# A deformable-convolution block: the sampling table stores a pixel and its step to the pixel below

## The chip, the cores and the metric

The kernel runs on one core of a Trainium2 chip. The metric is the device time of one execution in microseconds (us); lower is better. The median of nine executions of the kernel before is 8619.01 us, from 8593.27 to 8627.42 us. A profile is one further execution, taken by the hardware profiler. The names of the engines are those of the profile: PE is the matrix engine (PEld its weight loads), DVE the vector engine, ACT the scalar engine, POOL the engine that issues the indirect DMAs, SP the one that issues the plain DMAs.

## What is computed

The input is four images of 256 channels and 64 by 64 pixels in float32. The block first normalises over the channels and runs three modulated deformable 3x3 convolutions with a ReLU after each. The result is added to the input and goes through a mixture of eight experts, two per pixel. The change concerns the convolutions alone:

```python
om   = conv3x3(x, w_off) + b_off              # 27 numbers for each pixel
off  = om[:, :18].reshape(B, 9, 2, H, W); mask = sigmoid(om[:, 18:])
ys   = gy + base_y + off[:, :, 0];  xs = gx + base_x + off[:, :, 1]
y0, x0 = floor(ys), floor(xs);  wy, wx = ys - y0, xs - x0
# four gathered pixels, zero outside the image
v    = v00*(1-wy)*(1-wx) + v01*(1-wy)*wx + v10*wy*(1-wx) + v11*wy*wx
out  = relu(einsum('bikhw,oik->bohw', v * mask, w) + b)
```

For each of 9 taps and each pixel, 256 channels are read at a position between pixels, blended with bilinear weights and the mask, and multiplied by that tap's 256 by 256 weights.

## The kernel before

All data is float32. An image is worked in 8 blocks of 512 pixels (`BLK`), 8 image rows each; a block is 4 groups (`t`) of 128 pixels, one pixel per partition. The (layer, image) pairs are 12 stages: images 0 and 1 alternate through the three layers (stages 0 to 5), then images 2 and 3 (stages 6 to 11). So there are 96 blocks, 864 passes (block and tap `k`) and 3456 samples (block, tap and group).

**The table.** What is sampled lies in HBM as a table of (66 x 67) entries, one for each padded pixel. An entry has 512 numbers: the 256 channels of the pixel at (row, column) and, as its second half, those of the pixel one row below. Two entries that follow each other are therefore the four pixels of a bilinear sample. `store_table` (L160) writes a block with four DMAs from SP: for each half `d` of the rows, the pixels once as first halves and once, one row higher, as second halves. There are two tables per image parity, used by turns from layer to layer.

**Preparing.** `pre_block` (L170) loads 512 pixels of the input, transposes them (PE), normalises (DVE), stores the table, transposes back (PE) and copies into the padded image `xpad` (ACT). For images 0 and 1 this is the kernel's beginning; for images 2 and 3 its blocks are placed between the main blocks of stages 4 and 5. `off_block` (L197) runs the offset convolution from `xpad` on PE (L218), turns the result round (L231), and on DVE computes for 36 samples per pixel the table's index and four coefficients `cf` (L248 to L279). The off_block of a stage is placed between the main blocks of the stage ahead of it.

**The main block** (`main_block`, L281). For each tap and each group `t` (written a, b, c, d below), one indirect DMA from POOL (L296) brings two entries, 1024 numbers for each of 128 pixels, into one of 8 buffers `g`. ACT makes `s` by scaling the first 256 numbers (L303), one of 6 buffers. Three DVE multiply-adds of 256 numbers (`scalar_tensor_tensor`, L309) add the other three pixels. PE transposes `s` (L315) into a PSUM tile `tp`, of which there are 2. When the four groups of a tap are there, ACT copies them into `sT` in two instructions (L322), and PE multiplies with the tap's weights into the accumulator `acc` (L325). After nine taps ACT applies bias and ReLU (`r`, L335). In layers 0 and 1 DVE copies `r` into `xpad` (L338). PE transposes it back (`tpo`, L347, again a `tp` buffer), ACT copies that to `h` (L352, 2 buffers) and `store_table` writes the next layer's table. In layer 2 the input is added and `h` goes to HBM for the experts.

**The order.** Each engine works off its own list in order; the framework's scheduler makes the lists when the kernel is built, by priorities and its own estimates, so neighbouring taps overlap in it. In most passes of stages 0 to 3 and 6 to 11, DVE's list before has the three multiply-adds of a, then of b, c and d, and ACT's has the scaling of the next tap's a, then the two copies of L322, then the scalings of its b, c and d. In stages 4 and 5 the list of DVE mixes the samples for part of the taps (one multiply-add of a, one of b, and so on).

Of the kernel before, what the change touches and what calls it, by code (L numbers as in the profile page):

```python
# [14 lines left out]
P = 128  # L15
# [3 lines left out]
K = 9  # L19
# [71 lines left out]
def convolutions(ctx, tc, ins, x, B, dram, t_dram, ident, eps_c):  # L91
# [22 lines left out]
    for s in range(2):  # L114
        xp = cst.tile([P, CC, H + 2, W + 2], F32, name=f"xpad_{s}", tag=f"xpad_{s}")
        for c in range(CC):
            nc.vector.memset(xp[:, c, 0, :], 0.0)
            nc.vector.memset(xp[:, c, H + 1, :], 0.0)
            nc.vector.memset(xp[:, c, 1 : H + 1, 0:1], 0.0)
            nc.vector.memset(xp[:, c, 1 : H + 1, W + 1 : W + 2], 0.0)  # L120
        xpad.append(xp)
        for i in range(2):
            tb = dram.tile([TR * TC, 2 * C], F32, name=f"tab_{s}_{i}", tag=f"tab_{s}_{i}")
            v = tb.rearrange("(r c) (s f) -> r c s f", c=TC, s=2)
            nc.sync.dma_start(v[:, 0, :, :].rearrange("r s f -> r (s f)"), zero[:TR, : 2 * C])
# [43 lines left out]

    def pre_block(b, n):  # L170

        nm = f"pre_{b}_{n}"
        xc = work.tile([P, CC, BLK], F32, tag="xc", name=f"xc_{nm}")
        nc.sync.dma_start(xc, x[b, :, :, n * BLK : (n + 1) * BLK])
        tp = ps_t.tile([P, TPB, C], F32, tag="tp", name=f"tp_{nm}")
        for t in range(TPB):
            for c in range(CC):
                nc.tensor.transpose(
                    tp[:, t, c * P : (c + 1) * P], xc[:, c, t * P : (t + 1) * P], ident
                )  # L180
        h = work.tile([P, TPB, C], F32, tag="h", name=f"h_{nm}")
        normalise(nc, work, tp, h, eps_c, nm)
        store_table(table(0, b), h, n)
        tp2 = ps_t.tile([P, CC, BLK], F32, tag="tp", name=f"tp2_{nm}")
        for t in range(TPB):
            for c in range(CC):
                nc.tensor.transpose(
                    tp2[:, c, t * P : (t + 1) * P], h[:, t, c * P : (c + 1) * P], ident
                )
        for c in range(CC):  # L190
            nc.scalar.copy(
                rows(xpad[b % 2], c, n), tp2[:, c, :].rearrange("p (r w) -> p r w", w=W)
            )

    plans = {}

    def off_block(i, n):  # L197
# [6 lines left out]
        if n == 0:  # L204
            plans[i] = (
                work.tile([P, NB, J], I32, tag="idx", name=f"idx_{i}"),
                work.tile([P, NB, J, 4], F32, tag="cf", name=f"cf_{i}"),
            )
        idx, cf = plans[i]
        xp = xpad[b % 2]  # L210
# [64 lines left out]
        bm = small("bm", (P, J))  # L275
        nc.vector.tensor_tensor(bm, fr[:, 0, :], mk, ALU.mult)

        for q, (u, v) in enumerate(((am, om1), (bm, om1), (am, fr), (bm, fr))):
            nc.vector.tensor_tensor(cf[:, n, :, q], u, v[:, 1, :], ALU.mult)  # L279

    def main_block(i, n):  # L281
        l, b = stages[i]
# [5 lines left out]
        for k in range(K):  # L288
            tp = ps_t.tile([P, CC, BLK], F32, tag="tp", name=f"tp_{nm}_{k}")
            for t0 in range(0, TPB, 2):  # L290

                gs, ss = [], []
                for t in (t0, t0 + 1):
                    j = t * K + k
                    g = gat.tile([P, 4 * C], F32, tag="g", name=f"g_{nm}_{j}")
                    nc.gpsimd.indirect_dma_start(  # L296
                        out=g,
                        out_offset=None,
                        in_=tb,
                        in_offset=bass.IndirectOffsetOnAxis(ap=idx[:, n, j : j + 1], axis=0),  # L300
                    )
                    s = smp.tile([P, C], F32, tag="s", name=f"s_{nm}_{j}")
                    nc.scalar.activation(s, g[:, :C], AF.Copy, scale=cf[:, n, j, 0:1])  # L303
                    gs.append(g)
                    ss.append(s)
                for q in range(1, 4):
                    for u in range(2):
                        j = (t0 + u) * K + k
                        nc.vector.scalar_tensor_tensor(  # L309
                            ss[u], gs[u][:, q * C : (q + 1) * C], cf[:, n, j, q : q + 1], ss[u],  # L310
                            ALU.mult, ALU.add,
                        )
                for u in range(2):
                    for c in range(CC):
                        nc.tensor.transpose(  # L315
                            tp[:, c, (t0 + u) * P : (t0 + u + 1) * P],
                            ss[u][:, c * P : (c + 1) * P],
                            ident,
                        )
            sT = smT.tile([P, CC, BLK], F32, tag="sT", name=f"sT_{nm}_{k}")  # L320
            for c in range(CC):
                nc.scalar.copy(sT[:, c, :], tp[:, c, :])  # L322
            for c in range(CC):
                for o in range(CC):
                    nc.tensor.matmul(  # L325
                        acc[:, o, :],
                        lhsT=wk[:, k, c, o * P : (o + 1) * P],
                        rhs=sT[:, c, :],
                        start=(k == 0 and c == 0),
                        stop=(k == K - 1 and c == CC - 1),  # L330
                    )
# [19 lines left out]
        for t in range(0, TPB, 2):  # L351
            nc.scalar.copy(h[:, t : t + 2, :], tp[:, t : t + 2, :])  # L352
# [390 lines left out]
```

## Time and profile before

| | |
|---|---|
| time, median of 9 | 8619.01 us |
| time of the profiled execution | 8636.17 us |
| its span, first to last instruction | 8634.2 us |
| mean granted PE clock | 0.906 of full speed |
| beginning, to the first `sT` copy | 0 to 181 us |
| stages 0 to 11 | 181 to 6331 us |
| experts | from 6331 us |
| a stage of 72 passes, such as stage 1 (680 to 1176 us) | 496 us |
| stage 4 (2169 to 2756 us), stage 5 (2757 to 3331 us) | 587 us, 574 us |
| busy: PE, DVE, ACT, POOL | 6646.1, 5757.8, 3085.9, 4397.0 us |

The profile's page gives for each engine its busy time and how it is spread over 40 slices of the span, the granted PE clock and the DMA engines' load in the same slices, and the costliest groups of instructions. A group's row gives line, engine, operation, result and operands, shapes and count; then its total busy time and the mean duration of one in ns; then how long the engine stood idle just before such instructions and what ended that. The timeline lists instructions of a window: start, length, engine, line, and in brackets the idle time before and what ended it. Neighbours of one group are merged (xN). The waits are inferred from semaphores. Durations include the tail in which the result is written, so the next independent instruction can start before an instruction ends.

### The profile page before, as it was taken

What the parts mean: (1) busy time and instruction counts of PE and PEld (TensorE: products, weight loads), DVE (VectorE), ACT (ScalarE), POOL (GpSimd) and SP (SyncE); (2) the same over time, 40 slices, a digit from 0 to 9 for tenths busy, and PEclk for the clock granted to TensorE, in tenths of its full rate; (3) what the DMA queues carried; (4) which work ended last, traced back from release to release, by engine and by line L of the source; (5) the groups of instructions that cost most, each with busy time, mean ns of one, the idle gap of its engine ahead of it and who ended that gap; (6) DMA issues with size and microseconds to landing.
All of it is one profiled execution on the core that took longest, in us unless ns stands there. A gap on an engine that the chain in (4) does not pass through costs nothing.

```text
span 8634.2 us, 93574 instructions
## 1 busy us (share of the span) xinstructions
PE 6646.1 (77%) x25984; PEld 3678.5 (43%) x25984; DVE 5757.8 (67%) x14852; ACT 3085.9 (36%) x6658; POOL 4397.0 (51%) x4289
## 2 busy tenths in 40 slices
PE   7888888888877878888888888787753928658285
PEld 3434334433443433333343443343332827547274
DVE  5888888888777777888888887788862323323122
ACT  3444444444444444444444444444421212112011
POOL 1555565655555555555555555555523243433434
PEclk9999999999988889999999999889966969879697
DMA  7899999999888888999999999999932224333243
GB/s 234 315 326 318 325 334 322 323 319 326 309 294 295 302 295 319 325 323 327 318 335 324 319 322 336 347 327 326 321 140 80 92 93 129 113 100 121 82 128 122
DMA packets 791203, 2245.78 MB, mean 260 GB/s; under 512 B 131848, under 2 KB 244488, under 8 KB 789144
## 3 DMA queue, kind: packets, MB, share of 16 engines
q0 software_dynamic: 567168, 1917.26, 63.2%
q1 hardware_dynamic: 223512, 322.54, 11.1%
q8 instruction: 207, 3.39, 0.2%
q14 instruction: 316, 2.59, 0.1%
HBM read 2154.08 MB, written 231.78 MB: 276 GB/s over the span
## 4 chain that ended last, share of the span: by engine, by line
PE 38%; DVE 18%; issue 17%; DMA 15%; ACT 9%; POOL 2%; another core or an unknown queue 1%; ACTq 0%; SPq 0%; POOLq 0%; DVEq 0%
PE acc L325 15%; DVE s L309 15%; DMA g<-tab,idx 6%; PE tp L315 5%; DMA zs<-z,slots 5%; PE po L218 5%; PE ph L611 5%; PE py L626 4%; ACT sT L322 4%; ACT s L303 3%; DMA w<-in_W,wrow 3%; PE tpo L347 1%; POOL gy L650 1%; DMA gy<-ys,slots 1%
## 5 line engine op out<-in xcount | busy, mean ns | idle before, releaser
L309 DVE SCALAR_TENSOR_TENSOR s<-g,cf,s 128x256 f32<-128x256 f32 x10368 | 4711.6, 484 | 1049.2 <-ACT s L303 562.6
L296 POOL DMA_INDIRECT g<-tab,idx x3456 | 3586.1, 1038 | 2732.3 <-DVE s L309 1556.2
L325 PE MATMUL acc<-sT,wk 128*128 128x512 f32 x6912 | 3445.1, 645 | 405.4 <-ACT sT L322 317.1
L325 PEld LDWEIGHTS acc<-sT,wk 128*128 128x128 f32 x6912 | 1334.9, 203 | 2169.4 <-issue 1441.1
L322 ACT COPY sT<-tp 128x512 f32<-128x512 f32 x1728 | 927.7, 590 | 2516.8 <-PE tp L315 2195.3
L303 ACT ACTIVATE s<-g,cf 128x256 f32<-128x256 f32 x3456 | 1529.9, 510 | 394.7 <-DMA g<-tab,idx 241.9
L315 PE MATMUL tp<-ident,s 128*128 128x128 f32 x6912 | 1079.2, 284 | 434.2 <-DVE s L309 412.3
L315 PEld LDWEIGHTS tp<-ident,s 128*128 128x128 f32 x6912 | 819.2, 144 | 1159.8 <-DVE s L309 643.9
L585 POOL DMA_INDIRECT w<-in_W,wrow x312 | 312.2, 1001 | 858.4 <-ACT hT L620 341.7
L218 PE MATMUL po<-xpad,wo 128*32 128x512 f32 x3456 | 675.9, 610 | 1.9 <-DMA wo<-in_conv_w_off 1.0
L620 ACT ACTIVATE hT<-ph,w 128x256 f32<-128x256 f32 x624 | 258.7, 470 | 1164.2 <-PE ph L611 1080.5
L611 PE MATMUL ph<-fzT,w 128*128 128x256 f32 x2496 | 593.2, 393 | 65.2 <-DMA w<-in_W,wrow 64.7
L626 PE MATMUL py<-w,hT 128*128 128x256 f32 x2496 | 593.3, 393 | 57.4 <-DMA w<-in_W,wrow 45.1
L600 PE MATMUL ftp<-ident,zt 128*128 128x128 f32 x624 | 96.5, 284 | 619.6 <-DMA zt<-zs 610.1
L611 PEld LDWEIGHTS ph<-fzT,w 128*128 128x128 f32 x2496 | 483.9, 197 | 154.6 <-DMA w<-in_W,wrow 83.7
L626 PEld LDWEIGHTS py<-w,hT 128*128 128x128 f32 x2496 | 479.4, 197 | 134.7 <-issue 51.6
L572 POOL DMA_INDIRECT zs<-z,slots x256 | 251.6, 983 | 489.2 <-DMA zs<-z,slots 351.4
L634 DVE TENSOR_TENSOR y<-py,w 128x512 f32<-128x512 f32 x156 | 107.7, 691 | 490.2 <-PE py L626 448.5
L604 DVE COPY fzT<-ftp 128x512 f32<-128x512 f32 x156 | 107.5, 690 | 426.7 <-PE ph L611 272.5
L600 PEld LDWEIGHTS ftp<-ident,zt 128*128 128x128 f32 x624 | 76.9, 148 | 634.8 <-DMA zt<-zs 612.0
L650 POOL DMA_INDIRECT gy<-ys,slots x256 | 245.9, 960 | 148.4 <-issue 67.2
L658 DVE SCALAR_TENSOR_TENSOR facc<-gy,cw,facc 128x256 f32<-128x256 f32 x256 | 120.3, 483 | 222.1 <-DMA gy<-ys,slots 176.3
(122 smaller groups left out, 2567.0 us busy)
## 6 DMA issues: line engine op xcount, KB each, us to landing
tab<-h SPq DMA_DIRECT2D x256, 256.0 KB
g<-tab,idx POOLq DMA_INDIRECT x3456
zt<-zs SPq DMA_DIRECT2D x156, 256.0 KB
ys<-y SPq DMA_DIRECT2D x156, 256.0 KB
tab<-h_pre SPq DMA_DIRECT2D x128, 256.0 KB
zs<-nil SPq DMA_DIRECT2D x12, 1664.0 KB
xc_pre<-in_x SPq DMA_DIRECT2D x32, 512.0 KB
xr<-in_x SPq DMA_DIRECT2D x32, 512.0 KB
```

The source lines that it names most:

```text
L218: nc.tensor.matmul(po[g * Q : (g + 1) * Q, :], lhsT=wo[:, k, c, :], rhs=xp[:, c, RPB * n + ky : RPB * n + ky + RPB, kx : kx + W], start=(m ...
L296: nc.gpsimd.indirect_dma_start(out=g, out_offset=None, in_=tb, in_offset=bass.IndirectOffsetOnAxis(ap=idx[:, n, j : j + 1], axis=0),)
L303: nc.scalar.activation(s, g[:, :C], AF.Copy, scale=cf[:, n, j, 0:1])
L309: nc.vector.scalar_tensor_tensor(ss[u], gs[u][:, q * C : (q + 1) * C], cf[:, n, j, q : q + 1], ss[u], ALU.mult, ALU.add,)
L315: nc.tensor.transpose(tp[:, c, (t0 + u) * P : (t0 + u + 1) * P], ss[u][:, c * P : (c + 1) * P], ident,)
L322: nc.scalar.copy(sT[:, c, :], tp[:, c, :])
L325: nc.tensor.matmul(acc[:, o, :], lhsT=wk[:, k, c, o * P : (o + 1) * P], rhs=sT[:, c, :], start=(k == 0 and c == 0), stop=(k == K - 1 and c ...
L585: nc.gpsimd.indirect_dma_start(out=w, out_offset=None, in_=ins[src], in_offset=bass.IndirectOffsetOnAxis(ap=st["wrow"][:, f : f + 1], axis=0),
L611: nc.tensor.matmul(ph[:, h, :], lhsT=w1[:, o : o + P], rhs=zT[:, c, :], start=(c == 0), stop=(c == CC - 1),)
L620: nc.scalar.activation(hT[:, h0 + h, :], ph[:, h, :], AF.Gelu, bias=w1[:, k : k + 1])
L626: nc.tensor.matmul(py[:, u, :], lhsT=hT[:, h, u * P : (u + 1) * P], rhs=w2[:, h * C : (h + 1) * C], start=(h == 0), stop=(h == HC - 1),)
L650: nc.gpsimd.indirect_dma_start(out=g, out_offset=None, in_=ys[b % 2], in_offset=bass.IndirectOffsetOnAxis(ap=st["slots"][:, i, m : m + 1], ...
```

## The change

The second half of a table entry now holds the difference, pixel below minus pixel, in place of the pixel below. A sample then is: one multiply-add of 512 numbers that gives both columns' values at the fractional row (`v0 + wy * step`, written over `g`), one scaling of the left column on ACT by `(1-wx)*mask`, and one multiply-add of 256 numbers that adds the right column times `wx*mask`. There are three coefficients in place of four.

The differences are made by the new `store_steps`: a DVE subtraction over `xpad` (128 x 1024), eight transposes on PE into a `tp` buffer, two copies on ACT into a buffer of `h`'s pool, and the two DMAs that `store_table` no longer makes. It is called after `pre_block` has filled `xpad` and after the main blocks of layers 0 and 1, 32 + 64 = 96 times. In an image's last block it also makes the last row's step (minus the pixel), 12 times.

```diff
-            nc.sync.dma_start(v[H, 1 : W + 1, 1, :], zero[:W, :C])
...
-    def store_table(tb, h, n):
+    def store_table(tb, h, n, s):
         v = tb.rearrange("(r c) (s f) -> r c s f", c=TC, s=2)
         for d in range(2):
             src = h[d * W : (d + 1) * W, :, :]
-            for s in range(2):
-                r0 = RPB * n + d + 1 - s
-                dst = v[r0 : r0 + RPB - 1 : 2, 1 : W + 1, s, :]
-                nc.sync.dma_start(dst.rearrange("t x f -> x t f"), src)
+            r0 = RPB * n + d + 1 - s
+            dst = v[r0 : r0 + RPB - 1 : 2, 1 : W + 1, s, :]
+            nc.sync.dma_start(dst.rearrange("t x f -> x t f"), src)
+
+    def store_steps(tb, xp, n, nm):
+        dd = work.tile([P, CC, BLK], F32, tag="xc", name=f"dd_{nm}")
+        nc.vector.tensor_tensor(
+            dd.rearrange("p c (r w) -> p c r w", w=W),
+            xp[:, :, 1 + RPB * n : 1 + RPB * (n + 1), 1 : W + 1],
+            xp[:, :, RPB * n : RPB * (n + 1), 1 : W + 1],
+            ALU.subtract,
+        )
+        tp = ps_t.tile([P, TPB, C], F32, tag="tp", name=f"tpd_{nm}")
+        for t in range(TPB):
+            for c in range(CC):
+                nc.tensor.transpose(
+                    tp[:, t, c * P : (c + 1) * P], dd[:, c, t * P : (t + 1) * P], ident
+                )
+        hd = work.tile([P, TPB, C], F32, tag="h", name=f"hd_{nm}")
+        for t in range(0, TPB, 2):
+            nc.scalar.copy(hd[:, t : t + 2, :], tp[:, t : t + 2, :])
+        store_table(tb, hd, n, 1)
+        if n == NB - 1:
...
+            nc.sync.dma_start(v[H, 1 : W + 1, 1, :], hl[:W, 0, :])
...
-        store_table(table(0, b), h, n)
+        store_table(table(0, b), h, n, 0)
...
+        store_steps(table(0, b), xpad[b % 2], n, nm)
...
-        om1 = small("om1")
-        nc.vector.tensor_scalar(om1, fr, -1.0, 1.0, ALU.mult, ALU.add)
+        om1 = small("om1", (P, J))
+        nc.vector.tensor_scalar(om1, fr[:, 1, :], -1.0, 1.0, ALU.mult, ALU.add)
...
-        am = small("am", (P, J))
-        nc.vector.tensor_tensor(am, om1[:, 0, :], mk, ALU.mult)
-        bm = small("bm", (P, J))
-        nc.vector.tensor_tensor(bm, fr[:, 0, :], mk, ALU.mult)
-        for q, (u, v) in enumerate(((am, om1), (bm, om1), (am, fr), (bm, fr))):
-            nc.vector.tensor_tensor(cf[:, n, :, q], u, v[:, 1, :], ALU.mult)
+        nc.vector.tensor_copy(cf[:, n, :, 0], fr[:, 0, :])
+        nc.vector.tensor_tensor(cf[:, n, :, 1], om1, mk, ALU.mult)
+        nc.vector.tensor_tensor(cf[:, n, :, 2], fr[:, 1, :], mk, ALU.mult)
...
+                    v = g.rearrange("p (x s f) -> p x s f", x=2, s=2)
+                    nc.vector.scalar_tensor_tensor(
+                        v[:, :, 0, :], v[:, :, 1, :], cf[:, n, j, 0:1], v[:, :, 0, :],
+                        ALU.mult, ALU.add,
+                    )
                     s = smp.tile([P, C], F32, tag="s", name=f"s_{nm}_{j}")
-                    nc.scalar.activation(s, g[:, :C], AF.Copy, scale=cf[:, n, j, 0:1])
+                    nc.scalar.activation(s, v[:, 0, 0, :], AF.Copy, scale=cf[:, n, j, 1:2])
...
-                for q in range(1, 4):
-                    for u in range(2):
-                        j = (t0 + u) * K + k
-                        nc.vector.scalar_tensor_tensor(
-                            ss[u], gs[u][:, q * C : (q + 1) * C], cf[:, n, j, q : q + 1], ss[u],
-                            ALU.mult, ALU.add,
-                        )
+                for u in range(2):
+                    j = (t0 + u) * K + k
+                    nc.vector.scalar_tensor_tensor(
+                        ss[u], gs[u][:, 1, 0, :], cf[:, n, j, 2:3], ss[u], ALU.mult, ALU.add
+                    )
...
-            store_table(table(l + 1, b), h, n)
+            store_table(table(l + 1, b), h, n, 0)
+            store_steps(table(l + 1, b), xpad[b % 2], n, nm)
```

The lists that are built for the changed kernel, with A for the new 512-wide multiply-add, S for the scaling, B for the 256-wide multiply-add and T for the two copies of `sT`: in the later taps of most blocks DVE has A of a, A of b, B of a, B of b, A of c, B of c, A of d, B of d, and ACT has S of a, b, c, d and then T, so the next tap's S of a stands behind T. After a main block of layers 0 and 1 (that is, during tap 0 of the next block) ACT's list has the two copies of `h`, S of b of tap 1, the two copies of `hd`, then T of tap 0.

More of the change, by code (lines that the diff above doesn't have):

```diff
@@ L164, in store_table @@
             src = h[d * W : (d + 1) * W, :, :]
-            for s in range(2):
-                r0 = RPB * n + d + 1 - s
-                dst = v[r0 : r0 + RPB - 1 : 2, 1 : W + 1, s, :]
-                nc.sync.dma_start(dst.rearrange("t x f -> x t f"), src)
+            r0 = RPB * n + d + 1 - s
[20 more added lines that the diff above has]
+        if n == NB - 1:
+            dl = work.tile([P, CC, W], F32, tag="dl", name=f"dl_{nm}")
+            nc.vector.tensor_scalar(dl, xp[:, :, H, 1 : W + 1], -1.0, None, ALU.mult)
+            tp = ps_t.tile([P, TPB, C], F32, tag="tp", name=f"tpl_{nm}")
+            for c in range(CC):
+                nc.tensor.transpose(tp[:W, 0, c * P : (c + 1) * P], dl[:, c, :], ident)
+            hl = work.tile([P, TPB, C], F32, tag="h", name=f"hl_{nm}")
+            nc.scalar.copy(hl[:W, 0, :], tp[:W, 0, :])
+            v = tb.rearrange("(r c) (s f) -> r c s f", c=TC, s=2)
+            nc.sync.dma_start(v[H, 1 : W + 1, 1, :], hl[:W, 0, :])
     def pre_block(b, n):
@@ L206, in off_block @@
                 work.tile([P, NB, J], I32, tag="idx", name=f"idx_{i}"),
-                work.tile([P, NB, J, 4], F32, tag="cf", name=f"cf_{i}"),
+                work.tile([P, NB, J, 3], F32, tag="cf", name=f"cf_{i}"),
             )
@@ L301, in main_block @@
                     )
+                    v = g.rearrange("p (x s f) -> p x s f", x=2, s=2)
[3 more added lines that the diff above has]
+                    )
                     s = smp.tile([P, C], F32, tag="s", name=f"s_{nm}_{j}")
-                    nc.scalar.activation(s, g[:, :C], AF.Copy, scale=cf[:, n, j, 0:1])
-                    gs.append(g)
+                    nc.scalar.activation(s, v[:, 0, 0, :], AF.Copy, scale=cf[:, n, j, 1:2])
+                    gs.append(v)
                     ss.append(s)
-                for q in range(1, 4):
-                    for u in range(2):
-                        j = (t0 + u) * K + k
-                        nc.vector.scalar_tensor_tensor(
-                            ss[u], gs[u][:, q * C : (q + 1) * C], cf[:, n, j, q : q + 1], ss[u],
-                            ALU.mult, ALU.add,
-                        )
+                for u in range(2):
[3 more added lines that the diff above has]
+                    )
                 for u in range(2):
```

## Prediction

> **What bounds the kernel now.** I read the page first, for the shares and the groups, then the busy time by stage, then the timeline of an undisturbed pass and of the two kinds of block ends.
>
> ```profile
> DVE  5888888888777777888888887788862323323122
> ...
> PEclk9999999999988889999999999889966969879697
> DMA  7899999999888888999999999999932224333243
> ...
> L309 DVE SCALAR_TENSOR_TENSOR s<-g,cf,s 128x256 f32<-128x256 f32 x10368 | 4711.6, 484 | 1049.2 <-ACT s L303 562.6
> L296 POOL DMA_INDIRECT g<-tab,idx x3456 | 3586.1, 1038 | 2732.3 <-DVE s L309 1556.2
> ```
>
> Up to 6331 us DVE and the DMA engines are both near nine tenths. POOL waits for DVE (1556.2 us, for free `g` buffers), and L303's wait for gathers is only 241.9 us in all, so the DMA engines are full but gathers are seldom late. Where PEclk drops, PE's matmuls set the pass; the change does not touch those. Whether DVE's work bounds a pass is shown by the timeline (start, length, engine, line; count last).
>
> ```profile
> 3606.82 1.01 DVE L309 SCALAR_TENSOR_TENSOR s<-g,cf,s 128x256 f32<-128x256 f32 x2
> 3608.49 5.89 DVE L309 SCALAR_TENSOR_TENSOR s<-g,cf,s 128x256 f32<-128x256 f32 x12 [0.66 <-ACT sT L322]
> 3615.03 1.06 DVE L309 SCALAR_TENSOR_TENSOR s<-g,cf,s 128x256 f32<-128x256 f32 x2 [0.66 <-ACT sT L322]
> ```
>
> ```profile
> 3606.97 1.07 ACT L322 COPY sT<-tp 128x512 f32<-128x512 f32 x2 [3.88 <-PE tp L315]
> 3607.93 1.71 ACT L303 ACTIVATE s<-g,cf 128x256 f32<-128x256 f32 x4
> 3613.52 1.07 ACT L322 COPY sT<-tp 128x512 f32<-128x512 f32 x2 [3.88 <-PE tp L315]
> 3614.48 1.71 ACT L303 ACTIVATE s<-g,cf 128x256 f32<-128x256 f32 x4
> ```
>
> A pass is 6.55 us (3606.97 to 3613.52). It is a ring: T (the two copies), S (scalings), DVE's samples, transposes, T. DVE works 5.89 us of it and waits 0.66 us, each time for ACT. So DVE's work counts only as far as the ring shrinks.
>
> **Durations.** A 256-wide multiply-add lasts 484 ns; two on the same `s` start 0.52 us apart (1.01 us for two), two independent ones 0.40 (an independent pair takes 0.88 us at 1316.03). A sample of three is so 0.52 + 0.52 + 0.40 = 1.44 us. S lasts 0.51, the next starts 0.40 later. The trace has no 512-wide multiply-add out of SBUF. DVE's subtraction of 1024 numbers (L344) takes 1221 ns: (1221 - 484) / 768 = 0.96 ns a number, so A = 484 + 256 x 0.96 = 0.73 us. Ends: 0.69 (L634, 512-wide, 691 ns) and 0.97 (two of 484); I take 0.73, from the two rows of the same kind of operands.
>
> **The pass in the later taps (5 to 8), stages 0-3 and 6-11.** T at 0. Before, by those rows: S of b ends at 1.48, b's first multiply-add starts at 1.51, d's last ends at 5.92, and T comes 0.58 after that (3612.94 to 3613.52): 6.50, measured 6.55. After, S of a stands behind T and starts at 0.96 (A of a and b are done by then), ends 1.48; B of a 1.51, B of b 1.91, A of c 2.31 to 3.05, S of c to 3.59, B of c 3.62 to 4.11; A of d 4.02 to 4.76, S to 5.30, B 5.33 to 5.82; T at 6.40. The 0.39 us of DVE time saved per sample does not come out: samples c and d now hand over DVE to ACT to DVE, and nothing lies under that. 0.10 us x 4 passes x 80 blocks = **-32 us**. Ends: A at 0.97 makes two serial A's 0.24 longer each, +0.38 a pass; A at 0.69 makes it -0.18. The hand-over DVE to ACT I took as the 0.03 us of ACT to DVE (3615.00 to 3615.03); PE to ACT takes 0.09 (3613.43 to 3613.52), and with that the pass is 6.52.
>
> The Trainium skill (Perfetto Trace Analysis, Optimizing Scalar/DVE Operations) says larger operations pay if the engine is saturated, but that breaking instructions up may finish work sooner where the engine is not saturated and causes bubbles elsewhere. The second half speaks against this change in c and d: DVE idles while ACT scales, and by it A split in two would let S start about 0.25 us earlier twice, an estimate of 5.9 us a pass where the sum above has 6.40.
>
> **Ends of blocks in layers 0 and 1 (64).** Before:
>
> ```profile
> 3516.11 1.26 ACT L335 ACTIVATE r<-acc,bk 128x512 f32<-128x512 f32 x2 [2.11 <-PE acc L325]
> ...
> 3518.45 1.07 ACT L352 COPY h<-tpo 128x512 f32<-128x512 f32 x2 [0.67 <-PE tpo L347]
> 3519.41 1.09 ACT L322 COPY sT<-tp 128x512 f32<-128x512 f32 x2
> ```
>
> `r` ends at 3517.37; the two copies to `xpad` on DVE (429 ns) end about 3518.2. Added: subtraction 1.22 on DVE, eight transposes on PE (0.60 for four, so 1.04), copies of `hd` 1.07 on ACT. T of tap 0 stands behind `hd` and so comes near 3521.7, +2.2 us. Queued behind `hd` on ACT are T and the S's, and DVE's B's wait for those. Against it: the next passes (6.23, 7.4 and 6.65 us now) find A's done ahead, and DVE then needs only 4 x 1.05 = 4.2 us in them; PE needs 3.69 (eight L325) plus transposes and offset matmuls, about 5.3. They can win back 1 to 4 us. I take **0** per block, from -2 to +2.2: -128 to +141 us. It also takes a third `tp` tile per block end; that is in the +2.2.
>
> **Stages 4 and 5 (16 blocks).** These already last 587 and 574 us instead of 496, because a prepared block sits in each.
>
> ```profile
> 2458.84 0.30 ACT L82 ACTIVATE sd_pre<-mv_pre,eps_c 128x4 f32<-128x4 f32 x1 [1.54 <-DVE mv_pre L80]
> 2462.07 1.07 ACT L191 COPY xpad<-tp_pre 128x512 f32<-128x512 f32 x2 [2.93 <-PE tp_pre L187]
> 2463.03 0.92 ACT L303 ACTIVATE s<-g,cf 128x256 f32<-128x256 f32 x2
> 2463.84 1.07 ACT L322 COPY sT<-tp 128x512 f32<-128x512 f32 x2
> ```
>
> Subtraction, transposes and `hd` now come between the `xpad` copy and T of tap 0: 2463.14 + 1.22 + 1.04 + 1.07 + hand-overs = 2466.6 in place of 2463.84, +2.8 us. The later passes there take 5.5 us now,
>
> ```profile
> 2435.50 1.07 ACT L322 COPY sT<-tp 128x512 f32<-128x512 f32 x2 [3.23 <-PE tp L315]
> 2436.46 1.31 ACT L303 ACTIVATE s<-g,cf 128x256 f32<-128x256 f32 x3
> 2440.99 1.07 ACT L322 COPY sT<-tp 128x512 f32<-128x512 f32 x2 [3.23 <-PE tp L315]
> ```
>
> because the list mixes samples and the 0.40 us distance counts; the new list has the serial c and d of 6.40 us: +0.9 x 4. Together 6.4 x 16 = **+102 us**; ends 2.8 (gathers set those passes anyway) and 12 (`hd`, third tenant of two `h` buffers here, also waits for the store of the main block's `h`): +45 to +190.
>
> **The beginning (16 prepared blocks in 181 us).** The same chain, 3.3 us each, partly beside other blocks, with the `h` and `xc` buffers shared: 2.5 x 16 = **+40 us**, 0 to +56.
>
> **Small parts.** `hl`, 12 times, waits on ACT for the store of the same block's `h`: 1.5 us each, **+18**, 0 to +60. DVE's three fewer small operations per off_block (about 0.2 us, 96 times) lie in DVE's gaps: 0, down to -58. SP's DMAs keep number and bytes (half leave after `hd`, and the next stage but one reads them); one zero store per table goes. POOL's gathers keep number and bytes; a buffer comes free, as now, with its sample's last multiply-add.
>
> **Sum.** -32 + 0 + 102 + 40 + 18 = +128. Profiled execution: 8636.17 + 128 = 8764. It stood 17 above the median of the runs, so the predicted time is 8747 us.
>
> **Rivals.** *DVE's saving comes out (faster).* DVE's work falls by 10368 x 0.484 - 3456 x (0.73 + 0.484) = 822 us of durations, less 117 for 96 subtractions. For: DVE is 88% busy and POOL waits for it. Against: the list order above. It decides if taps 1 to 4 keep a run-ahead and take about 5.8 us: -0.8 x 4 x 80 = -256, so 8747 - 256 = about 8490.
> *The hand-overs or a tail cost more.* With 0.09 instead of 0.03 and one extra wait of that kind, +0.18 us in each of 864 passes: +155, about 8900.
> *The 512-wide one costs like two (0.97).* +0.48 a pass over my 6.40, on 864 passes: +415, about 9160.
> *Gathers set the time anyway.* Bytes are unchanged, and the DMA share in the stages is 0.92: within 0.2%, 8619. Against: L303's small wait for gathers.
>
> **How the numbers follow.** Chances: my sum 0.57, saving comes out 0.18, hand-overs 0.12, width 0.06, gathers 0.07. About 0.2% (17 us) is what a measurement tells from no change. Of the 0.57, 0.55 lies above that: slower 0.73, same 0.09, faster 0.18. The sum's own range from its ends is 8640 to 8900; with half of the faster case and the hand-overs the range is 8540 to 8940.
>
> **What would show it.** Right: A near 730 ns, DVE busy lower by some 600 us yet with more idle behind L335 (the new scaling); passes of 5 to 8 at 6.4 to 6.5 us; tap 0's T two us later; stages 4 and 5 longer by 50 us each. Wrong: passes at 5.8 or less in the later taps (hand-overs overlap after all), or A near 0.97.

## The result, and the profile after

The changed kernel takes 8684.92 us (median of 10 runs, 8660.53 to 8697.73); the kernel before took 8620.64 us beside it (8593.27 to 8641.05). The ratio is 1.0076, interval 1.0066 to 1.0086: slower by 64 us, where 128 were forecast. On a second chip (below) the ratio is 1.0098, interval 1.0081 to 1.0115. The profiled execution took 8707.08 us, span 8705.1, granted clock 0.905 as before.

From the page of the changed kernel: busy tenths of DVE and of the DMA engines, then groups (busy time, mean ns of one, idle time before them and what ended most of it).

```profile
DVE  4677767776666666777777777566661323323122
...
DMA  5899999999888888999999999999942224333243
...
L323 POOL DMA_INDIRECT g<-tab,idx x3456 | 3628.0, 1050 | 2761.7 <-DVE s L340 1818.7
...
L340 DVE SCALAR_TENSOR_TENSOR s<-g,cf,s 128x256 f32<-128x256 f32 x3456 | 1608.7, 483 | 1659.6 <-ACT s L335 1395.6
L330 DVE SCALAR_TENSOR_TENSOR g<-g,cf 128x512 f32<-128x512 f32 x3456 | 2519.8, 746 | 91.0 <-DMA g<-tab,idx 82.5
L335 ACT ACTIVATE s<-g,cf 128x256 f32<-128x256 f32 x3456 | 1679.9, 511 | 1930.8 <-DVE g L330 1423.7
```

The change did what its words say: A (L330, the 512-wide multiply-add) lasts 746 ns, B (L340) 483, and DVE is busy 5058.9 us in place of 5757.8. But 699 us less work bought nothing. DVE's idle time behind ACT's scaling (S) rose from 562.6 to 1395.6 us, and ACT's scalings now wait 1423.7 us for the multiply-add A, where the kernel before shows 55.5 us of waiting for DVE at its scalings. The timeline of a pass of the later taps (start, length, engine, line) shows the two waits facing each other, first DVE:

```profile
3652.89 0.88 DVE L340 SCALAR_TENSOR_TENSOR s<-g,cf,s 128x256 f32<-128x256 f32 x2 [0.77 <-ACT sT L352]
3653.69 0.75 DVE L330 SCALAR_TENSOR_TENSOR g<-g,cf 128x512 f32<-128x512 f32 x1
3655.01 0.48 DVE L340 SCALAR_TENSOR_TENSOR s<-g,cf,s 128x256 f32<-128x256 f32 x1 [0.57 <-ACT s L335]
3655.41 0.74 DVE L330 SCALAR_TENSOR_TENSOR g<-g,cf 128x512 f32<-128x512 f32 x1
3656.73 0.48 DVE L340 SCALAR_TENSOR_TENSOR s<-g,cf,s 128x256 f32<-128x256 f32 x1 [0.58 <-ACT s L335]
```

then ACT in the same pass:

```profile
3651.38 1.07 ACT L352 COPY sT<-tp 128x512 f32<-128x512 f32 x2 [1.10 <-issue]
3652.34 0.92 ACT L335 ACTIVATE s<-g,cf 128x256 f32<-128x256 f32 x2
3654.47 0.51 ACT L335 ACTIVATE s<-g,cf 128x256 f32<-128x256 f32 x1 [1.22 <-DVE g L330]
3656.19 0.51 ACT L335 ACTIVATE s<-g,cf 128x256 f32<-128x256 f32 x1 [1.21 <-DVE s L340]
3657.80 1.07 ACT L352 COPY sT<-tp 128x512 f32<-128x512 f32 x2 [1.11 <-issue]
```

The pass is 6.42 us (3651.38 to 3657.80) against 6.55 before. A of c ends at 3654.44, S of c runs from 3654.47 to 3654.98, B of c starts at 3655.01: 0.03 us each way, with nothing on DVE in between. DVE idles 0.77 + 0.57 + 0.58 us of the pass.

The end of a block, ACT's part of it:

```profile
3675.03 1.26 ACT L365 ACTIVATE r<-acc,bk 128x512 f32<-128x512 f32 x2 [0.78 <-PE acc L355]
...
3678.23 1.07 ACT L382 COPY h<-tpo 128x512 f32<-128x512 f32 x2 [0.27 <-PE tpo L377]
...
3680.25 1.07 ACT L185 COPY hd<-tpd 128x512 f32<-128x512 f32 x2
3681.38 1.07 ACT L352 COPY sT<-tp 128x512 f32<-128x512 f32 x2
```

From `r` to the copies of tap 0 (T) it was 3.30 us in the block end that the prediction shows, and is 6.35 in this one. Where the time of the two profiled executions lies, by the first `sT` copies of the stages:

| | before | after | difference |
|---|---|---|---|
| beginning, to the first T | 181.1 | 262.1 | +81.0 |
| stages 0 to 3 and 6 to 9 | 3970.7 | 3952.0 | -18.7 |
| stages 4 and 5 | 1162.9 | 1197.1 | +34.2 |
| stages 10 and 11 | 1017.5 | 993.0 | -24.5 |
| after the last T | 2302.0 | 2300.9 | -1.1 |

In layer 2 (stages 10 and 11), where no steps are made, the change gains; it loses where the steps of layer 0 are made, in the beginning and in stages 4 and 5.

### The profile page after: what moved, and what is told of

It is laid out like the page before. It is cut to its first block, busy times and chain, and to the rows that moved or that the text cites. A ratio compares the mean times of both kernels' runs of the same rounds, so it can differ in the third digit from the quotient of the medians.

```text
span 8705.1 us, 91686 instructions
## 1 busy us (share of the span) xinstructions
PE 6745.2 (77%) x26776; PEld 3762.3 (43%) x26776; DVE 5058.9 (58%) x11216; ACT 3349.3 (38%) x6860; POOL 4439.9 (51%) x4289
## 4 chain that ended last, share of the span: by engine, by line
PE 25%; issue 13%; DMA 10%; ACT 8%; DVE 7%; POOL 2%; another core or an unknown queue 0%; ACTq 0%; POOLq 0%; SPq 0%; DVEq 0%
PE acc L355 9%; ACT s L335 5%; DMA zs<-z,slots 5%; PE ph L642 4%; PE py L657 4%; DVE g L330 3%; DMA w<-in_W,wrow 3%; PE tp L345 2%; PE po L248 2%; ACT sT L352 2%; DVE s L340 1%; DMA gy<-ys,slots 1%; DMA g<-tab,idx 1%; POOL gy L681 1%; POOL zs L603 1%
## 5 line engine op out<-in xcount | busy, mean ns | idle before, releaser
L323 POOL DMA_INDIRECT g<-tab,idx x3456 | 3628.0, 1050 | 2761.7 <-DVE s L340 1818.7
L355 PE MATMUL acc<-sT,wk 128*128 128x512 f32 x6912 | 3401.4, 638 | 413.2 <-ACT sT L352 257.7
L340 DVE SCALAR_TENSOR_TENSOR s<-g,cf,s 128x256 f32<-128x256 f32 x3456 | 1608.7, 483 | 1659.6 <-ACT s L335 1395.6
L330 DVE SCALAR_TENSOR_TENSOR g<-g,cf 128x512 f32<-128x512 f32 x3456 | 2519.8, 746 | 91.0 <-DMA g<-tab,idx 82.5
L335 ACT ACTIVATE s<-g,cf 128x256 f32<-128x256 f32 x3456 | 1679.9, 511 | 1930.8 <-DVE g L330 1423.7
L345 PE MATMUL tp<-ident,s 128*128 128x128 f32 x6912 | 1029.6, 281 | 342.9 <-DVE s L340 225.1
L248 PE MATMUL po<-xpad,wo 128*32 128x512 f32 x3456 | 716.4, 627 | 37.8 <-ACT xpad L220 19.6
```

The costliest lines, as they stand in the source:

```text
L248: nc.tensor.matmul(po[g * Q : (g + 1) * Q, :], lhsT=wo[:, k, c, :], rhs=xp[:, c, RPB * n + ky : RPB * n + ky + RPB, kx : kx + W], start=(m ...
L323: nc.gpsimd.indirect_dma_start(out=g, out_offset=None, in_=tb, in_offset=bass.IndirectOffsetOnAxis(ap=idx[:, n, j : j + 1], axis=0),)
L330: nc.vector.scalar_tensor_tensor(v[:, :, 0, :], v[:, :, 1, :], cf[:, n, j, 0:1], v[:, :, 0, :], ALU.mult, ALU.add,)
L335: nc.scalar.activation(s, v[:, 0, 0, :], AF.Copy, scale=cf[:, n, j, 1:2])
L340: nc.vector.scalar_tensor_tensor(ss[u], gs[u][:, 1, 0, :], cf[:, n, j, 2:3], ss[u], ALU.mult, ALU.add)
L345: nc.tensor.transpose(tp[:, c, (t0 + u) * P : (t0 + u + 1) * P], ss[u][:, c * P : (c + 1) * P], ident,)
```

## The experiments

The expectations give times on the scale of the chip of the result (8620 before). The experiments ran on other chips, where the kernel before takes 8493 to 8502 us (8620 in the last one), so they are compared by their ratio to the runs of before on the same chip. This table has them all. Behind the ratio it gives, from the profiles (us), the first T, stages 0 to 3 and 6 to 9 together, 4 and 5, 10 and 11, the usual (median) pass behind taps 4 to 7 in the eight stages (from that tap's copies to the next), and the usual step from T of tap 8 to T of the next tap 0.

| kernel | ratio, interval | first T | 0-3, 6-9 | 4, 5 | 10, 11 | pass | block end |
|---|---|---|---|---|---|---|---|
| before, again | 1 | 174.1 | 3932.4 | 1075.5 | 1007.8 | 6.55 | 7.68 |
| changed, again | 1.0098, 1.0081 to 1.0115 | 263.9 | 3915.8 | 1104.7 | 998.0 | 6.42 | 10.56 |
| without layer 0's steps | 0.9957, 0.9940 to 0.9974 | 177.7 | 3942.0 | 1033.9 | 990.8 | 6.43 | 10.56 |
| without the later steps | 1.0061, 1.0044 to 1.0079 | 264.4 | 3875.2 | 1102.0 | 1000.9 | 6.43 | 8.34 |
| A in two halves | 0.9790, 0.9772 to 0.9809 | 262.8 | 3721.8 | 1104.8 | 935.3 | 5.90 | 10.56 |
| no hand-over | 0.9514, 0.9498 to 0.9530 | 259.0 | 3577.4 | 1079.0 | 863.1 | 5.30 | 10.53 |
| changed, a pair ahead | 1.0098, 1.0081 to 1.0115 | 262.6 | 3933.5 | 1117.0 | 977.0 | 5.3 to 5.9 | 10.56 |
| before, a pair ahead | 0.9497, 0.9476 to 0.9519 | 178.1 | 3598.5 | 1108.2 | 901.0 | 5.30 | 8.34 |
| own buffers | 0.9990, 0.9977 to 1.0003 | 217.8 | 3881.0 | 1086.1 | 989.9 | 6.42 | 10.55 |
| one sample behind | 0.9529, 0.9513 to 0.9545 | 271.0 | 3585.6 | 1082.1 | 889.9 | 5.30 | 10.56 |
| both of these | 0.9427, 0.9408 to 0.9446 | 224.7 | 3560.5 | 1066.2 | 889.9 | 5.30 | 10.56 |
| before, scalings ahead | 0.9802, 0.9779 to 0.9825 | 182.7 | 3838.4 | 1123.0 | 1003.0 | 5.4 to 6.5 | 8.09 |

**What the steps cost.** Two kernels leave them out, once in the prepared blocks and once at the ends of the main blocks.

```diff
+            nc.sync.dma_start(v[H, 1 : W + 1, 1, :], zero[:W, :C])
...
 # in pre_block; the second kernel does the same in main_block, with table(l + 1, b)
-        store_steps(table(0, b), xpad[b % 2], n, nm)
+        store_table(table(0, b), h, n, 1)
```

> Left out: the steps of layer 0's tables (32 prepared blocks: subtraction, transposes, copies to hd, and hl four times); the lower half of layer 0's table gets the pixel below instead of the step, stored from h with the same bytes and number of stores, so layer 0's samples are not the reference's. All else is the changed kernel. My sum priced these steps at 40 (beginning) + 102 (stages 4 and 5) + 6 (hl) = 148 us: 8685 - 148 = 8537. The two traces say 81 (the first copy of a tap comes at 262.1 instead of 181.1) and 34 (15.7 + 18.5), 115 in all: 8570. If the beginning's loss were something else than the steps' own chain (the stores' order, the gathers), the beginning stays at 262 and the time above 8640.

> Left out: the steps of the tables of layers 1 and 2 (64 block ends: subtraction, eight transposes, two copies to hd, and hl eight times); the lower half of those tables gets the pixel below, stored from h, so the samples of layers 1 and 2 are not the reference's. All else is the changed kernel. My sum: the block ends cost 0 net (-128 to +141) and hl 8 x 1.5 = 12: 8673, within 20 us of the changed kernel. Rival: the first copy of tap 0 comes 3 to 4.6 us later in the changed kernel (the interval from tap 8 to the next tap 0 is 10.8 to 12.3 us instead of 8.6 plus what is regained), and if nothing of it were truly won back, taking the steps away gives 64 x 3.4 = 218 us: 8467. In between, the share that is not won back is read from the time.

Layer 0's steps: 0.9957 against 1.0076 to 1.0098 for the changed kernel is 1.2 to 1.4%, 101 to 120 us, as the traces said (115) and less than my sum (148). The beginning is back at 177.7; stages 4 and 5 are 71 us shorter than in the changed kernel and 42 shorter than in the kernel before. So in those stages the steps cost 71 and the new sampling gives 42 back. The later 64 steps: 13 to 31 us by the ratios, where I had 12. Without them T of tap 0 comes 8.34 us after tap 8's, with them 10.56: +2.22, the forecast's figure. And the intervals of taps 0 to 3 give it back: they sum to 25.88 us without the steps and 22.71 with them. These are medians; by the means the end takes 2.56 us more and the taps 0 to 3 give back 1.83. The eight stages are 41 us longer with the steps (3915.8 against 3875.2, on two of the quicker chips), and 36 of these are PE's waits for `hl` (below), so the rest of the 64 block ends costs about 5 us.

**The hand-over.** The first kernel splits A, the left column first, so that S can start after the first half; the second lets S read a column that A does not write.

```diff
-                        v[:, :, 0, :], v[:, :, 1, :], cf[:, n, j, 0:1], v[:, :, 0, :],
+                        v[:, 0, 0, :], v[:, 0, 1, :], cf[:, n, j, 0:1], v[:, 0, 0, :],
+                        ALU.mult, ALU.add,
+                    )
+                    nc.vector.scalar_tensor_tensor(
+                        v[:, 1, 0, :], v[:, 1, 1, :], cf[:, n, j, 0:1], v[:, 1, 0, :],
```

```diff
-                    nc.scalar.activation(s, v[:, 0, 0, :], AF.Copy, scale=cf[:, n, j, 1:2])
+                    nc.scalar.activation(s, v[:, 0, 1, :], AF.Copy, scale=cf[:, n, j, 1:2])
```

> The 512-wide multiply-add is two of 256, the left column first, and the scaling on ScalarE needs the left one alone; the sums are the same. VectorE again has three 256-wide ones a sample: 3456 x (2 x 484 - 746) = 767 us more of durations. Hand-over theory (a pass of the later taps is the ring of copy, scaling, multiply-adds, transposes, with c and d handed over serially): S of c and of d starts about 0.26 us earlier, twice a pass, pass 5.9 instead of 6.42, 80 blocks x 4 passes x 0.5 = 160 us and something in the other passes: 8525, that is faster than before (8620). Rival, VectorE's work sets the pass: slower, above 8750. Rival, gathers set it: 8685, pass unchanged at 6.4.

> ScalarE scales the step of the left column, which the 512-wide multiply-add reads and does not write, so the scaling no longer waits for VectorE; the sample lacks the left pixel, so the output is not the reference's. Number, size and engine of all work are as in the changed kernel. Hand-over theory: the scalings are done ahead, as before the change, and the pass of the later taps falls from 6.42 to what is next: VectorE's 4 x (0.65 + 0.40) = 4.2, TensorE about 5.1, gathers 5.4 (the passes of stage 4): 5.5 to 5.8, 80 x 4 x 0.75 = 240 us: about 8445, 8350 to 8520. Rival, VectorE's work or the gathers set the pass: 8685 within 20, pass unchanged.

More DVE work, less time: with three 256-wide multiply-adds a sample again, the split kernel beats both kernels (0.979). DVE in the split kernel, one pass:

```profile
3834.26 0.48 DVE L330 SCALAR_TENSOR_TENSOR g<-g,cf 128x256 f32<-128x256 f32 x1
3834.66 0.48 DVE L334 SCALAR_TENSOR_TENSOR g<-g,cf 128x256 f32<-128x256 f32 x1
3835.31 0.48 DVE L344 SCALAR_TENSOR_TENSOR s<-g,cf,s 128x256 f32<-128x256 f32 x1 [0.18 <-ACT s L339]
```

The right half now lies under S, and DVE's wait for S of c and of d is 0.18 us in place of 0.57. The pass is 5.90, as expected (5.9). The total gain (2.8 to 3.1% of the changed kernel, about 250 us) is above my 160: 194 us in the eight stages and 63 in stages 10 and 11. The granted clock rose too: in stages 10 and 11 from 0.90 and 0.93 to 0.94 and 0.98, in the other eight from 0.95-0.98 to 0.99-1.00. What part of the gain outside the usual passes is the clock's was not separated. Without the hand-over the pass falls to 5.30, below the 5.5 to 5.8 I gave it, and the ratio to 0.951. DVE's work as the bound of the old pass, and the gathers as its bound, are both out: neither became less.

**The order of the lists.** If the hand-over costs only because nothing lies under it, the order is at fault. Two kernels put the sampling a pair of samples ahead and force it by issue-order edges: the changed kernel and, as a control, the kernel before.

```diff
...
 # changed kernel: load() gathers a pair and issues its A's and S's, and returns the last A
+        waiting = None
+        for k in range(K):
+            for t0 in range(0, TPB, 2):
+                loaded, last = load(k, t0)
+                if waiting is not None:
+                    finish(*waiting, last)      # B's of the waiting pair behind `last`
+                waiting = loaded
...
```

```diff
...
 # kernel before: load() issues the S's of a pair; finish() of the waiting pair
             for q in range(1, 4):
                 for u in range(2):
-                        nc.vector.scalar_tensor_tensor(
+                    with tc.issue_after(behind.ins) if behind is not None else ExitStack():
+                        behind = nc.vector.scalar_tensor_tensor(
...
+            with tc.issue_after(scaled.ins) if scaled is not None else ExitStack():
                 for c in range(CC):
                     nc.scalar.copy(sT[:, c, :], tp[:, c, :])
```

> The changed kernel once more, beside the next two kernels on their chip, so that stages are compared on one chip: the kernel before runs 8495 on the chip of the first four experiments and 8621 on that of the result. All theories: 1.0076 times the kernel before (1.0066 to 1.0086).

> The changed kernel with its sampling in pairs one ahead: the gathers, 512-wide multiply-adds and scalings of the next pair stand before the 256-wide multiply-adds of this pair, and that order is forced on VectorE by issue-order edges (A a, A b, B c, B d of the tap before, A c, A d, B a, B b). Work, sizes and sums are those of the changed kernel. Hand-over theory: between A and B of a sample lie two or more other multiply-adds (1.0 to 1.4 us), more than the hand-over's 0.58 us, so the pass falls from 6.42 to what the kernel without the hand-over showed (5.30 to 5.4 in taps 4 to 8): its time over that of before was 0.951; here 0.95 to 0.965. Rival, the pass is set by VectorE's or TensorE's work and the kernel without the hand-over was fast because it left the wait and a dependence out: 0.99 or more.

> The same order forced on the kernel before: scalings of the next pair before the copies of a tap on ScalarE, and the six 256-wide multiply-adds of a pair alternating between its two samples on VectorE, so that two on the same sample never follow each other. Work, sizes and sums are those of the kernel before. If the old kernel's pass of 6.55 was its order (0.52 us between dependent multiply-adds, S behind T) and not VectorE's work, 12 x 0.40 = 4.8 us of VectorE fit and the pass falls to 5.3 to 5.6, ratio 0.95 to 0.97: then fewer multiply-adds are worth nothing that the order could not give. If VectorE's work set it (5.9 of 6.55 us busy), the pass stays above 6.2 and the ratio above 0.98, and the change's fewer multiply-adds are worth what e7 gains over this one.

The control is the surprise. The kernel before, with not one instruction less, runs in 0.9497 of its time: its DVE, busy for 4975 of the 6150 us of the stages (81%) and for 5.89 of the 6.55 us of the usual pass (90%), was no bound. In its usual pass nothing is left but PE's work and one wait for T:

```profile
3686.05 3.70 PE L335 MATMUL acc<-sT,wk 128*128 128x512 f32 x8 [0.73 <-ACT sT L332]
3689.59 1.04 PE L322 MATMUL tp<-ident,s 128*128 128x128 f32 x8
3691.36 0.70 PE L335 MATMUL acc<-sT,wk 128*128 128x512 f32 x1 [0.73 <-ACT sT L332]
```

In the changed kernel the same idea gained nothing (1.0098). Its waits (time, times, longest):

```profile
DVE g L329 <- DMA g<-tab,idx: 1446.1, 1635, 8.3
```

In the changed kernel itself this wait is 82.5 us (87.7 in its second profile). A pair ahead keeps up to four of the eight `g` buffers between A and B; the quiet passes did fall to 5.30, but taps 0 to 2 rose to 6.57, 7.76 and 6.76 us (from 5.41, 5.63 and 5.50) while A waited for gathers. That these were late for want of a free buffer is the likely reading, since POOL waits 1622.1 us for DVE there; a kernel with more buffers was not run.

**One sample behind, and buffers for the steps.** So the next order holds one sample only: A b, B a, A c, B b, A d, B c, A of the next tap's a, B d. The other kernel gives the steps buffers of their own: `dd` takes the tag of `r`, `hd` and `hl` a buffer each (room for it comes from a smaller `zero`). A third does both.

```diff
...
+                loaded, last = load(k, t)           # one sample
+                if waiting is not None:
+                    finish(*waiting, last)          # its B behind `last`
...
```

```diff
-        dd = work.tile([P, CC, BLK], F32, tag="xc", name=f"dd_{nm}")
+        dd = work.tile([P, CC, BLK], F32, tag="r", name=f"dd_{nm}")
...
-        hd = work.tile([P, TPB, C], F32, tag="h", name=f"hd_{nm}")
+        hd = step.tile([P, TPB, C], F32, tag="hd", name=f"hd_{nm}")
...
-            hl = work.tile([P, TPB, C], F32, tag="h", name=f"hl_{nm}")
+            hl = step.tile([P, C], F32, tag="hl", name=f"hl_{nm}")
```

> The changed kernel with each 256-wide multiply-add forced behind the 512-wide one of the next sample on VectorE (A b, B a, A c, B b, A d, B c, A a of the next tap, B d), instead of the pairs of the earlier run, which held four gather buffers between A and B and came out at 1.0098 with waits of 1446 us for gathers. Work, sizes and sums are the changed kernel's. Hand-over theory with buffers: a sample is held for one other multiply-add only (0.65 us, more than the 0.58 us of the hand-over), no gather is late, the pass of taps 4 to 8 is TensorE's 5.30 and the early taps are near those of the kernel without the hand-over: ratio 0.950 to 0.965. Rival, the changed kernel cannot have the order without late gathers, since VectorE must finish the first multiply-add before ScalarE and both hold the buffer longer than before: the early taps stay at 6.5 to 7.5 us and the ratio is 0.98 or more.

> The changed kernel with buffers of their own for the steps: dd takes the r tag (idle while blocks are prepared), hd and hl a buffer each, so h and xc alternate over two buffers again. Work, order in the program and sums are the changed kernel's. The trace of the changed kernel shows ACT idle before hd_pre with no releaser named (91 us over 26 times) and three waits of hl for a store of h of 13 us each. Buffer theory: h and hd take turns in two buffers, so each h waits for the store of the h before, one block earlier; with buffers of their own the first copy of a tap comes at 185 to 205 instead of 264, and the three waits of hl go (-36): together 95 to 120 us off, ratio to the kernel before 0.996 to 0.999. Rival, the chain of work itself (subtraction, transposes, copies, in the engines' lists behind the offsets) is the price: the beginning stays above 245 and the gain is the hl waits alone, ratio 1.005.

> The buffers of their own and the order one sample behind together; work and sums are the changed kernel's. If the two causes are separate, the gains add: by the buffer and hand-over theories 0.935 to 0.950, below the kernel before with its order forced (0.9497). If the block ends or the prepared blocks are set by TensorE or by the gathers in the new order, less than the sum.

One sample behind gives 0.9529, and A's wait for gathers falls from 1446.1 to 272.4 us. The matmul row of its later pass shows what is left:

```profile
3730.82 3.70 PE L355 MATMUL acc<-sT,wk 128*128 128x512 f32 x8 [0.73 <-ACT sT L352]
3734.36 1.04 PE L345 MATMUL tp<-ident,s 128*128 128x128 f32 x8
3736.13 0.70 PE L355 MATMUL acc<-sT,wk 128*128 128x512 f32 x1 [0.73 <-ACT sT L352]
```

PE's eight matmuls, the eight transposes behind them and the wait for T's first copy fill the 5.30 us (3730.82 to 3736.13). The ordered kernel before has the same 5.30, and its ratio, 0.9497, is no worse. Little room lies below: in stages 0 to 3 the DMA engines are busy for 0.96 to 0.97 of the time in the kernel one sample behind, 0.91 to 0.93 in the changed kernel.

Buffers of their own bring the changed kernel level with the kernel before (0.9990). The waits of `hl` (48.2 us in the second profile of the changed kernel) are gone. The beginning fell by 46 us, not by 59 to 79: prepared blocks follow each other in 12.5 us on average instead of 16.3, and in the kernel before in 10.6. So the buffers are about half of the beginning's loss; which of `dd` and `hd` it is, and what the other 44 us are, was not separated. Both changes together give 0.9427, where taking the two gains off 1.0098 gives 0.942. That kernel is the fastest here: 8027.60 us against 8502.42 for the kernel before on that chip.

**The two halves of the control.** The ordered kernel before differs from the old one in two things; this one has its scalings ahead of T, but three multiply-adds on the same sample in a row, as of old.

```diff
 # against the ordered kernel before
-            for q in range(1, 4):
-                for u in range(2):
+            for u in range(2):
+                for q in range(1, 4):
```

> The kernel before with its scalings in pairs ahead of the copies of a tap on ScalarE, as in the run with its order forced (ratio 0.9497), but with VectorE's multiply-adds sample by sample, three on the same sample in a row, as in the kernel before. Work and sums are those of the kernel before. It tells the two halves of that order apart. If the ring over the copies set the old pass (6.55), it falls to VectorE's own 4 x 1.44 = 5.76 (0.52 + 0.52 + 0.40 a sample), 5.8 to 5.9 in taps 4 to 8, and the ratio is 0.965 to 0.975: VectorE's work is then the second bound, met only once the ring is cut, and the rest to 0.9497 is the distance of dependent multiply-adds. If the scalings' place is nothing and only that distance counted, the pass stays near 6.5 and the ratio above 0.99. If the distance is nothing, 0.95.

The ratio is 0.9802, a little above the expected range, mainly since the pass after tap 0 rose from 6.23 to 7.66 us (1.4 us in each of 64 blocks, about 1%). The usual pass behind taps 5 and 6 is 5.75 (5.37 behind tap 4, 6.45 behind tap 7). DVE's timeline over two passes is one line, 26 multiply-adds with no gap:

```profile
3863.65 12.51 DVE L316 SCALAR_TENSOR_TENSOR s<-g,cf,s 128x256 f32<-128x256 f32 x26
```

In these passes DVE's work is the bound: 24 multiply-adds in 2 x 5.75 us are 0.48 each, the mean of 0.52, 0.52 and 0.40. Alternating samples brings that to 0.40 x 12 = 4.8, and PE's 5.30 takes over.

> The kernel before, profiled on the same chip, for its stages: the same time as its other runs, within 0.3%.

That run took 8472.57 us, its neighbours 8492.63.

## Why the prediction was right, and where not

- **The ring as the bound: right, and shown.** Shortening the hand-over while adding DVE work made the kernel faster (0.9790); taking S off the ring in the kernel before did too (0.9802). Three bounds lie behind one another: ring 6.55 (new ring 6.42), DVE 5.75, PE 5.30. The change lowered the middle one. The prediction's 88% for DVE stands in no row (81% of the stages, 90% of the usual pass); it entered a rival, not the sum.
- **The later passes, 6.40: measured 6.42.** A was estimated at 0.73 us and lasts 0.746. The -32 us came to -36 in the ten stages of the two profiles (by the usual passes, 26.2 to 25.7 us for four, it would be -40).
- **The ends of blocks, 0 net: right.** T of tap 0 comes 2.22 us later by the steps, and taps 0 to 3 win it back. In stages 0 to 3 and 6 to 9 the two profiles differ by -18.7 us; less the 36 of `hl` and the -22 of the later passes, -33 us are left for block ends and taps 0 to 3, -0.5 per block. That it is won back because A's and B's done ahead leave DVE less to do is argued, not tested.
- **Stages 4 and 5, +102: measured +34. This step failed.** Its term "+0.9 x 4" took one pass of 5.5 us as the pass of taps 4 to 7 there. The mean of the old profile is 24.4 us for four, 6.1 each, and the new one 23.7: the 6.40 us of the new order show only behind taps 6 and 7 (6.24 and 6.53), while those behind taps 4 and 5 take 5.46. The other term was too small: from T of tap 8 to the next tap 0 the mean went from 17.73 to 23.94, +6.2 against my +2.8. But the catching up that I allowed at the other block ends I left out here: taps 0 to 3 fell from 30.6 to 27.2. Two wrong sizes and one omission.
- **The beginning, +40: measured +81.** The step charged 2.5 us a block, for a chain of 3.3 that lies partly beside other blocks. The loss is 5 us a block, more than the whole chain. `hd` and `dd` take every other turn in the two buffers of `h` and `xc`, and blocks came to stand mostly 14.5 to 16 us apart; own buffers took 46 us off. The 44 that stay are near the 40 of the sum; that they are the chain was not tested. The changed kernel's timeline shows one block and the start of the next:

```profile
60.67 0.30 ACT L82 ACTIVATE sd_pre<-mv_pre,eps_c 128x4 f32<-128x4 f32 x1 [2.30 <-DVE mv_pre L80]
...
65.84 1.22 DVE L171 TENSOR_TENSOR dd_pre<-xpad 128x1024 f32<-128x1024 f32 x1 [1.64 <-ACT xpad L220]
...
68.38 1.07 ACT L185 COPY hd_pre<-tpd_pre 128x512 f32<-128x512 f32 x2 [2.57 <-issue]
...
72.08 1.09 PE L207 MATMUL tp_pre<-ident,xc_pre 128*128 128x128 f32 x8
...
75.16 0.30 ACT L82 ACTIVATE sd_pre<-mv_pre,eps_c 128x4 f32<-128x4 f32 x1 [2.30 <-DVE mv_pre L80]
```

- **`hl`, +18: measured 36 on PE, and not 1.5 us each.** Three of the twelve wait 13 to 14 us, the others 2 us or less. They are those at the start of stages 2, 4 and 8. The waits of `hl` and for it (us in total, times, longest):

```profile
ACT hl L195 <- DMA tab<-h: 46.6, 8, 14.1
PE tp L345 <- ACT hl L195: 36.3, 3, 12.9
```

  SyncE's queue in the changed kernel, start of stage 2:

```profile
1230.37 0.37 SPq L151 DMA_DIRECT2D wk<-in_conv_w  x1
1233.82 8.31 SPq L166 DMA_DIRECT2D tab<-h  x2
1242.22 7.05 SPq L166 DMA_DIRECT2D tab<-hd  x2
1255.08 0.48 SPq L197 DMA_DIRECT2D tab<-hl  x1
```

  The next layer's weights (2304 KB) are issued ahead of the store of `h`; `hl` waits on ACT for that store, since it takes its buffer, and T, S and the transposes stand behind it. The Trainium skill (DMA: Bandwidth & Descriptors, Queues, rings and completion order) says that each DMA engine takes a queue's descriptors in ring order; the 8.31 us that the two stores of `h` take in SyncE's queue here fit that, against 1.23 us for the two stores of a prepared block. Only these three of the main blocks' `hl` come behind a load of weights; no run moved that load, so this cause is argued. What is shown is that `hl` waits for the store of `h`, and that the waits go with a buffer of its own. The sum's 1.5 us had no load ahead of the store.
- **The sum: part of its nearness is luck.** The two profiles differ by 71 us. Measured less forecast, the terms missed by -4 (later passes), -33 (block ends and early taps), -68 (stages 4 and 5), +41 (beginning) and +18 (`hl`); -11 in the early taps of stages 10 and 11, for which the sum had no term, and -1 after the last T make up the rest. Without the two misses upwards (beginning and `hl`) the forecast would have been twice as far off. The sum's own range, 8640 to 8900, is also narrower than the ends beside its terms give: taken as independent misses they make about 8590 to 8980.
- **The rivals.** "DVE's saving comes out" needed passes of 5.8 in taps 1 to 4: taps 1 and 2 came at 5.65 and 6.10, taps 3 and 4 at 6.37 and 6.42, and the longer block ends took most of that gain. "The hand-overs cost more" is out with 0.03 us each way, "512-wide costs like two" with 746 ns, and "gathers set the time" with the passes of 5.30 at the same bytes.
- **The rule weighed in the prediction.** By the second half of it (the Trainium skill, Perfetto Trace Analysis, Optimizing Scalar/DVE Operations: break instructions up where an unsaturated engine makes others wait) the estimate was 5.9 us a pass; the split measured 5.90. Its first half, larger operations for a saturated engine, fits here the kernel with scalings ahead, where DVE has no gaps; no run tried A in that setting alone.

## What to carry to other kernels

Here an engine that was busy for 90% of the repeating pass was not its bound; its wait inside the pass (0.66 us, for ACT) was the sign. Look for the ring through the other engines before cutting instructions: with the same instructions, moving the work that closes the ring ahead gave 2% here, and alternating the samples on DVE 3% more. A change that turns a scaling of loaded data into a scaling of a result adds a hand-over; order the list so that another sample's work lies under it, and count how many buffers that order holds. Work that borrows a double buffer's tag takes turns from the old tenant (own buffers gave about 1% here): look what each waits for, and what is queued ahead of that store.

## What was not expected of the hardware

The same kernel before takes 8620 to 8621 us beside the result and beside the last experiment, and 8493 to 8502 us on the three other chips, 1.5% less. In the profiles of 8636.17 and 8472.57 us, 87 of the 164 us lie in stages 4 and 5 (1162.9 and 1075.5 us), 38 in the other stages of layers 0 and 1 and 21 after the last T; the granted clock is 0.906 and 0.912. What makes that difference stays open. The price of the steps in stages 4 and 5 (71 us) was measured on two of the quicker chips, against each other.
